# Collecting routed experts with sums taken in the last addition, squares on ScalarE and one Sqrt per step; the last W update left out

## The chip, the cores and the metric

The kernel runs on one core of a Trainium2 chip. All data are float32. The metric is the device time of that core in microseconds (us), and the time of a kernel is the median of its runs. For the kernel before it is 2762.55 us, the median of 3 runs between 2755.8 and 2763.34 us. One further execution was recorded by the hardware profiler: it took 2751.21 us, and its profile spans 2749.3 us of that.

## The reference

The input is 2 sequences of 4096 tokens of width 512. Two layers follow each other, each closed by a residual sum and a layer norm.

The first layer ("attention") is a recurrence per sequence. With k, v and q three projections of each token, it holds a matrix W (512x512) and a bias b, and per token computes

```
g = 2/512 * (W @ k + b - v)
W = W - 0.01 * outer(g, k);   b = b - 0.01 * g
out = W @ q + b
x = layernorm(x + out)
```

Only `out` leaves the recurrence. The W and b that stand after the last token are used by nothing.

The second layer is a mixture of 8 experts with hidden width 256. Every token goes through a shared expert, and through the 2 experts of 8 for which sqrt(softplus(logit)) is largest, weighted by that value:

```
y = shared(x) + sum over the 2 chosen e of  c_e * (silu(x @ W1_e + b1_e) @ W2_e + b2_e)
out = layernorm(x + y)
```

A layer norm here subtracts the mean of the 512 values of a token and divides by the root of their variance plus 1e-5.

## The kernel before, in words

**Steps.** The recurrence is done in 32 steps of 128 tokens of both sequences (`step(c)`, c = 0 to 31, lines 392 to 470). Within a step the 128 token updates are solved at once: `prep(c)` projects K and Q and forms small 128x128 matrices (L304, L317), `invert(c)` inverts their 32x32 diagonal blocks on VectorE (L347), `join(c)` joins the blocks to the full inverse in levels. A level is four matmuls into `pz` (L384) and one VectorE addition that gives the tile Z (L386); the next level multiplies Z again, so it can't start before that addition has ended. The last Z is called Y. Then come the right side R (L402 to L412), the output `po` (L422), transposes of K (`pk`, L437, copied to K by VectorE, L439), the solved update `pe` = Y times R (L446), F as its scaled copy by ScalarE (L448), the output's second part (L452), and the update of W (matmuls `pw` L457, additions L458) and of the bias (`pb` L463, L464).

**Shared expert and router.** `shared(c)` (lines 555 to 632) runs one step later: transposes, the shared expert, the router, whose activations are Exp, Ln, Silu and Sqrt on ScalarE, and a write of x plus the shared part to a DRAM table `gb`, which is the base that the routed experts are added to.

**Routed experts.** Steps 0 to 22 are group a and steps 23 to 30 group b. When a group's last step has been routed, `plan` sorts its tokens by expert into tiles of 128 rows. `routed(gr)` (lines 764 to 830) works the tiles off, 99 for a and 39 for b. Per tile k, GpSimd issues two gathers by DMA, the tokens `g` (L771) and the expert's weights `wb` (L777, 3 buffers, so those of tile k+3 wait until tile k has been read by the VectorE addition `o`, L809). TensorE transposes the tokens (`pg` L786; copied to gT by ScalarE, L788), multiplies (`phe` L795), ScalarE applies Silu (`he` L799), and TensorE multiplies again (`pye` L806). The result goes to the DRAM table `ge`.

**Collecting.** `collect(gr)` (lines 832 to 873) finishes the output of one step of the group at a time: `fetch` issues on GpSimd's queue the load of the base `acc` (L839, 3 buffers) and four gathers of routed rows, `z` (L845, 2 buffers each). VectorE adds the four weighted rows (L862, two per sequence); then `layernorm` (lines 273 to 291) does for each of the two sequences bn_stats (L276), bn_aggr (L278), an addition of eps (L280), Sqrt on ScalarE (L281), a reciprocal (L283), a product (L286) and the normalizing Identity on ScalarE (L287). ScalarE's queue then issues the write of `acc` to the output (L872). `fetch` for the next collected step is issued ahead of a collected step's additions.

**The last step's tokens** (c = 31) go through all 8 experts without sorting, in `dense` (lines 649 to 681), at the end.

**What sets the order.** The order of instructions on TensorE and VectorE is the order in which the program is written (L884 says so); the order on the other engines is chosen by the scheduler of the language. `interleave` (L63) mixes several generators: each yields an amount of work, and the one that is furthest behind its share goes on. In steps 28 to 31 group a's collecting is one of the parts, with an amount from `COLLECTED` (5, 5, 5 and 3 collected steps) and held back for the first part of the step (L900, L901). After step 31, tiles of b, the shared part of step 31 and the rest of a's collecting are mixed (L910); at the very end `dense` and the collecting of b (L913).

Of the kernel before, what the change touches and what calls it, by code (L numbers as in the profile page):

```python
# [40 lines left out]
F32 = mybir.dt.float32  # L41
# [60 lines left out]
def postln_block(ctx: ExitStack, tc: tile.TileContext, x, xT, thK, thV, thQ, w0, b0, masks, blk,  # L102
# [289 lines left out]
    def step(c):  # L392
# [25 lines left out]
        for s in range(B):  # L418
# [13 lines left out]
            if s == 0:  # L432

                for r in range(B):
                    ps = ps_s.tile([P, DC, P], F32, tag="ps", name=f"pk_{c}_{r}")
                    for ec in range(DC):
                        nc.tensor.transpose(ps[:, ec, :], KQ[:, ec, r, 0, :], ident)  # L437
                    k = stepp.tile([P, DC, P], F32, tag="K", name=f"K_{c}_{r}")
                    nc.vector.tensor_copy(k, ps)  # L439
                    K.append(k)  # L440
                    if r == 0:
                        Y = next(levels)
                    yield 1.5
        for s in range(B):
            ps = ps_s.tile([P, D], F32, tag="ps", name=f"pe_{c}_{s}")
            nc.tensor.matmul(ps, Y[:, s, :], R[s], start=True, stop=True)  # L446
            f = stepp.tile([P, D], F32, tag="F", name=f"F_{c}_{s}")
            nc.scalar.mul(f, ps, -BETA)  # L448
            F.append(f)
            yield 3.0  # L450
        for s in range(B):
# [3 lines left out]
            for ec in range(DC):  # L455
                ps = ps_s.tile([P, D], F32, tag="ps", name=f"pw_{c}_{s}_{ec}")
                nc.tensor.matmul(ps, K[s][:, ec, :], F[s], start=True, stop=True)  # L457
                nc.vector.tensor_tensor(W[s][:, ec, :], ps, W[s][:, ec, :], ALU.add)  # L458
                if s > 0 and ec == 1:
                    next(norm[0])  # L460
                yield 1.0
            ps = ps_s.tile([P, D], F32, tag="ps", name=f"pb_{c}_{s}")
            nc.tensor.matmul(ps, ones, F[s], start=True, stop=True)  # L463
            nc.vector.tensor_tensor(brep[s], ps, brep[s], ALU.add)  # L464
            yield 1.0
# [183 lines left out]
    def dense(c):  # L649
# [4 lines left out]
        for e in range(E + 1):  # L654
            if e < E:
                w = dense_w[e]
                h_e[e] = stepp.tile([P, HC, T], F32, tag="F", name=f"hd_{e}")
# [106 lines left out]
    def routed(gr):  # L764
# [17 lines left out]
        def turn(k):  # L782
# [4 lines left out]
            gT[k] = gp.tile([P, DC, P], F32, tag="gT", name=f"gT_{gr.g}_{k}", bufs=1)  # L787
# [43 lines left out]

    def collect(gr):
# [18 lines left out]

        fetch(0)
        yield 2.0
        for j in range(gr.n):
# [4 lines left out]
            norm = []  # L859
            for s in range(B):  # L860
                for k in range(K):
                    nc.vector.scalar_tensor_tensor(acc[:, s, :], z[s * K + k],  # L862
                                                   gr.cw[:, j, s, k:k + 1], acc[:, s, :],
                                                   ALU.mult, ALU.add)
                    yield 0.8
                norm.append(layernorm(acc, "f", c, s, scalar=True))
                next(norm[s])
                yield 0.4
                if s > 0:
                    next(norm[s - 1])  # L870
            next(norm[B - 1])
            nc.scalar.dma_start(out=out[:, c * P:(c + 1) * P, :].rearrange("s p d -> p s d"),  # L872
                                in_=acc)
# [7 lines left out]
    COLLECTED = {NCH - 4: 5, NCH - 3: 5, NCH - 2: 5, NCH - 1: 3}  # L881
# [5 lines left out]
    for c in range(NCH):  # L887
# [11 lines left out]
        if c > spread[-1]:  # L899
            amount = COLLECTED[c] * COLLECT  # L900
            parts.append((1.5 * amount, held(part_of(collects[0], amount), 0.25 * amount)))  # L901
# [4 lines left out]
        if c == NCH - 2:  # L906
            dense_weights(2)
    dense_weights(1 + B + 2)
    next(tiles[1])
    interleave([(b.tiles * TILE, tiles[1]), (60.0, shared(NCH - 1)),  # L910
                ((a.n - sum(COLLECTED.values())) * COLLECT, collects[0])])
    dense_weights(E - len(dense_w))
# [70 lines left out]
```

## Time and profile before

The profiled execution took 2751.21 us and its profile spans 2749.3 us. The stages around the change, by the times at which their first matmuls start:

| stage | us from the span's start | length |
|---|---|---|
| a step without routed work (step 16) | 1011.0 to 1072.6 | 61.6 |
| step 28 | 2164.5 to 2235.8 | 71.3 |
| step 29 | 2235.8 to 2306.2 | 70.4 |
| step 30 | 2306.2 to 2381.6 | 75.4 |
| step 31 | 2381.6 to 2459.4 | 77.8 |
| tiles of group b, with the rest of a's collecting | 2459.4 to 2670.1 | 210.7 |
| dense experts, with the collecting of b | 2670.1 to 2749.3 | 79.2 |

Durations of instructions that matter, as means of the profile: the weighted addition (L862) 757 ns, bn_stats 687, bn_aggr 182, the eps addition 153, the reciprocal 157, the product L286 214, a Sqrt 203, a normalizing Identity 805, a load of ScalarE's function table 1283, an indirect DMA on GpSimd about 1000 to 1075 with 300 between two, and the direct load of acc 767.

How to read it: PE is TensorE, PEld its weight loads, DVE VectorE, ACT ScalarE, POOL GpSimd. A table of stretches gives for each stretch its length, then busy time (and instructions) of PE, PEld, DVE, ACT and POOL, the granted share of TensorE's clock, the DMA engines' busy share and GB/s. In a timeline, each line is a start, a duration, engine, line and operation; a bracket at the end is the idle time before it and what ended it. In a list of waits, "A <- B: t, n, m" says that A waited for B for t us in total, n times, at most m.

### The profile page before, as it was taken

Reading aid. Unit: us, or ns where it says so; the run is one execution under the profiler, and the core shown is the slowest. Engines: PE = TensorE matmul, PEld = TensorE weight load, DVE = VectorE, ACT = ScalarE, POOL = GpSimd, SP = SyncE. Lnnn points to the kernel's source line nnn. Section 1 sums busy time; section 2 is a strip of 40 time slices with the busy share of each in tenths; the row PEclk is TensorE's granted clock in tenths of the full one; section 3 lists DMA queues with packets and bytes.
Section 4 is the critical chain, followed back from the end, with each engine's and each line's share of the span. In section 5 each row is a group of like instructions: output and inputs, shape, how many; then the busy total and the mean of one; then the engine's idle time right before and its main releaser. Section 6 shows DMA issues by size and latency. Waiting matters only on the chain.

```text
span 2749.3 us, 31544 instructions
## 1 busy us (share of the span) xinstructions
PE 2629.7 (96%) x10593; PEld 1683.8 (61%) x10593; DVE 1327.9 (48%) x4189; ACT 767.4 (28%) x1493; POOL 763.5 (28%) x767
## 2 busy tenths in 40 slices
PE   8999999999999999999999999999999989878886
PEld 6656666666656666666555766767676655445664
DVE  2455554455555555454556223232232588753228
ACT  1222222222222222232222322323133233414447
POOL 0111111111111111112113333342333354454445
PEclk9999999999999999999999999999999999889998
DMA  4112111111111111111113343452434365575566
GB/s 162 36 64 63 48 41 49 40 40 40 42 61 47 42 42 47 40 40 40 46 57 112 113 108 97 115 163 82 122 99 96 117 193 181 188 248 170 194 208 225
DMA packets 148785, 269.38 MB, mean 98 GB/s; under 512 B 61180, under 2 KB 62940, under 8 KB 145040
## 3 DMA queue, kind: packets, MB, share of 16 engines
q1 hardware_dynamic: 90608, 139.50, 15.5%
q0 software_dynamic: 49584, 111.61, 14.1%
q10 hardware_dynamic: 8432, 16.25, 1.6%
q8 instruction: 85, 1.39, 0.2%
q14 instruction: 76, 0.62, 0.1%
HBM read 333.37 MB, written 88.64 MB: 153 GB/s over the span
## 4 chain that ended last, share of the span: by engine, by line
PE 85%; DMA 4%; issue 4%; DVE 4%; ACT 2%; POOL 1%; SPq 0%; POOLq 0%; DVEq 0%; ACTq 0%
PE pkq L304 16%; PE pye L806 8%; PE pr L402 8%; PE pr L407 8%; PE po L422 8%; PE phe L795 7%; PE pw L457 7%; PE ph L582 4%; PE py L621 4%; PE pa L317 3%; PE pb L463 2%; PE pg L786 2%; PE po L452 2%; PE pe L446 2%; PE pz L384 1%
## 5 line engine op out<-in xcount | busy, mean ns | idle before, releaser
L347 DVE SCALAR_TENSOR_TENSOR X<-L,X 128x31 f32<-128x31 f32 (+22 forms) x1472 | 330.9, 270 | 26.2 <-DMA L<-dL 9.2
L795 PEld LDWEIGHTS phe<-gT,wb 128*128 128x128 f32 x2208 | 270.9, 194 | 66.0 <-issue 61.9
L809 DVE TENSOR_TENSOR o<-pye,wb 128x512 f32<-128x512 f32 x138 | 95.4, 691 | 424.3 <-PE pye L806 409.1
L806 PE MATMUL pye<-wb,he 128*128 128x512 f32 x552 | 269.8, 612 | 28.6 <-ACT he L799 20.5
L795 PE MATMUL phe<-gT,wb 128*128 128x128 f32 x2208 | 273.6, 278 | 11.9 <-DMA wb<-wcat_in,widx 10.4
L549 POOL DMA_INDIRECT gt<-code,ri x124 | 123.8, 998 | 548.9 <-DVE ri L546 518.5
L457 PE MATMUL pw<-F,K 128*128 128x512 f32 x512 | 246.8, 605 | 8.7 <-DVE x L453 6.8
L304 PE MATMUL pkq<-xT,thQ 128*128 128x256 f32 x1024 | 245.6, 384 | 9.8 <-DVE Z L386 9.8
L304 PE MATMUL pkq<-xT,thK 128*128 128x256 f32 x1024 | 243.6, 382 | 7.4 <-DMA thK<-thK_in 7.4
L422 PE MATMUL po<-W,kq 128*128 128x512 f32 x512 | 245.9, 604 | 0.0
L304 PEld LDWEIGHTS pkq<-xT,thK 128*128 128x128 f32 x1024 | 195.9, 192 | 71.6 <-issue 49.0
L402 PE MATMUL pr<-thV,xT 128*128 128x512 f32 x512 | 239.3, 599 | 0.0
L777 POOL DMA_INDIRECT wb<-wcat_in,widx x138 | 142.4, 1032 | 347.9 <-DVE o L809 191.7
L407 PE MATMUL pr<-W,kq 128*128 128x512 f32 x512 | 231.9, 592 | 0.0
L304 PEld LDWEIGHTS pkq<-xT,thQ 128*128 128x128 f32 x1024 | 187.2, 191 | 36.1 <-DVE Z L386 10.3
L799 ACT ACTIVATE he<-phe,wb 128x128 f32<-128x128 f32 x276 | 86.4, 363 | 417.0 <-PE phe L795 359.5
L458 DVE TENSOR_TENSOR W<-pw,W 128x512 f32<-128x512 f32 x256 | 173.5, 688 | 57.0 <-PE pw L457 52.9
L311 ACT COPY kq<-pkq 128x256 f32<-128x256 f32 x256 | 83.1, 375 | 390.3 <-PE pkq L304 383.9
L806 PEld LDWEIGHTS pye<-wb,he 128*128 128x128 f32 x552 | 99.2, 191 | 131.6 <-issue 90.2
L771 POOL DMA_INDIRECT g<-gy,gidx x138 | 138.5, 1004 | 146.2 <-PE pg L786 109.5
L457 PEld LDWEIGHTS pw<-F,K 128*128 128x128 f32 x512 | 94.0, 191 | 136.2 <-issue 96.7
L845 POOL DMA_INDIRECT z<-ge,sidx x124 | 133.3, 1075 | 117.7 <-DVE acc L862 40.4
(199 smaller groups left out, 3446.5 us busy)
## 6 DMA issues: line engine op xcount, KB each, us to landing
ge<-o SPq DMA_DIRECT2D x138, 256.0 KB
xT<-xT_in SPq DMA_DIRECT2D x32, 512.0 KB
x<-x_in SPq DMA_DIRECT2D x32, 512.0 KB
L<-dL SPq DMA_DIRECT2D x128, 128.0 KB
gy<-x SPq DMA_DIRECT2D x31, 512.0 KB
gb<-x SPq DMA_DIRECT2D x31, 512.0 KB
acc<-gb POOLq DMA_DIRECT2D x31, 512.0 KB
y_out<-acc ACTq DMA_DIRECT2D x31, 512.0 KB
```

Of the source, the lines that this page charges most:

```text
L304: nc.tensor.matmul(ps[:, i].rearrange("p s t -> p (s t)"), th[:, dc, (ec + i) * P:(ec + i + 1) * P], xt[:, dc].rearrange("p s t -> p (s t) ...
L347: nc.vector.scalar_tensor_tensor(X[:, h, j + 1:], L[:, j + 1:, j], X[:, h, j:j + 1], X[:, h, j + 1:], ALU.mult, ALU.add)
L402: nc.tensor.matmul(ps, xt[:, dc, s, :], nthV_sb[:, dc, :], start=(dc == 0), stop=False)
L407: nc.tensor.matmul(ps, KQ[:, ec, s, 0, :], W[s][:, ec, :], start=False, stop=(ec == DC - 1))
L422: nc.tensor.matmul(ps, KQ[:, ec, s, 1, :], W[s][:, ec, :], start=(ec == 0), stop=False)
L457: nc.tensor.matmul(ps, K[s][:, ec, :], F[s], start=True, stop=True)
L458: nc.vector.tensor_tensor(W[s][:, ec, :], ps, W[s][:, ec, :], ALU.add)
L771: nc.gpsimd.indirect_dma_start(out=g_t[k], out_offset=None, in_=gr.y, in_offset=bass.IndirectOffsetOnAxis(ap=gr.gidx[:, k:k + 1], axis=0), ...
L777: nc.gpsimd.indirect_dma_start(out=wbuf[k % NW], out_offset=None, in_=wcat, in_offset=bass.IndirectOffsetOnAxis(ap=gr.widx[:, k:k + 1], ax ...
L795: nc.tensor.matmul(ps[:, hc, :], w[:, dc * HF + hc * P:dc * HF + (hc + 1) * P], t[:, dc, :], start=(dc == 0), stop=(dc == DC - 1))
L806: nc.tensor.matmul(ps, h[:, hc, :], w[:, O2 + hc * D:O2 + (hc + 1) * D], start=(hc == 0), stop=(hc == HC - 1))
L845: nc.gpsimd.indirect_dma_start(out=t, out_offset=None, in_=gr.ex, in_offset=bass.IndirectOffsetOnAxis(ap=gr.sidx[:, j, s, k:k + 1], axis=0 ...
```

## The change

In `collect`, sums come out of the second weighted addition of a sequence itself (`accum_out`), the squares and their sums from two ScalarE activations, and eps, Sqrt, reciprocal and product are done for both sequences at once. The part from eps on is a generator, `finish`, that runs among the additions of the collected step after it. A flag, `squares`, turns this off for the stage of group b's tiles: there bn_stats and bn_aggr stay, still with one Sqrt, and VectorE does the normalizing.

In `step`, the last step has no transposes of K and no update of W and bias; the last level of `join` is issued ahead of the first transposes of K in every step; F takes the place of R. In `dense` a tile takes R's buffers in place of F's; gT has 2 buffers in place of 1. `COLLECTED` falls from 5, 5, 5, 3 to 3, 3, 3, 1 collected steps, and the collecting's amount and hold in a step change.

```diff
                 for r in range(B):
+                    if r == 0:
+                        Y = next(levels)
+                    if c == NCH - 1:
+                        continue
                     ps = ps_s.tile([P, DC, P], F32, tag="ps", name=f"pk_{c}_{r}")
                     for ec in range(DC):
                         nc.tensor.transpose(ps[:, ec, :], KQ[:, ec, r, 0, :], ident)
                     k = stepp.tile([P, DC, P], F32, tag="K", name=f"K_{c}_{r}")
                     nc.vector.tensor_copy(k, ps)
                     K.append(k)
-                    if r == 0:
-                        Y = next(levels)
                     yield 1.5
...
-            f = stepp.tile([P, D], F32, tag="F", name=f"F_{c}_{s}")
-            nc.scalar.mul(f, ps, -BETA)
-            F.append(f)
+            nc.scalar.mul(R[s], ps, -BETA)
+            F.append(R[s])
...
-            for ec in range(DC):
-                ps = ps_s.tile([P, D], F32, tag="ps", name=f"pw_{c}_{s}_{ec}")
...
+            if c < NCH - 1:
+                for ec in range(DC):
+                    ps = ps_s.tile([P, D], F32, tag="ps", name=f"pw_{c}_{s}_{ec}")
...
+            elif s > 0:
+                next(norm[0])
...
-            gT[k] = gp.tile([P, DC, P], F32, tag="gT", name=f"gT_{gr.g}_{k}", bufs=1)
+            gT[k] = gp.tile([P, DC, P], F32, tag="gT", name=f"gT_{gr.g}_{k}")
...
+        def finish(c, acc, mean, var, on_scalar):
+            if on_scalar:
+                nc.vector.tensor_scalar(var, var, 1.0 / D, EPS, ALU.mult, ALU.add)
+            else:
+                nc.vector.tensor_scalar(var, var, EPS, None, ALU.add)
+            nc.scalar.activation(var, var, AF.Sqrt)
+            yield
+            nc.vector.reciprocal(var, var)
+            if on_scalar:
+                nc.vector.tensor_tensor(mean, mean, var, ALU.mult)
+            for s in range(B):
+                if on_scalar:
+                    nc.scalar.activation(acc[:, s, :], acc[:, s, :], AF.Identity,
+                                         bias=mean[:, s:s + 1], scale=var[:, s:s + 1])
+                else:
+                    nc.vector.tensor_scalar(acc[:, s, :], acc[:, s, :], mean[:, s:s + 1],
+                                            var[:, s:s + 1], ALU.subtract, ALU.mult)
+            nc.scalar.dma_start(out=out[:, c * P:(c + 1) * P, :].rearrange("s p d -> p s d"),
+                                in_=acc)
+            yield
...
+            on_scalar = squares[0]
+            mv = sm.tile([P, 2, B], F32, tag="fmv", name=f"fmv_{c}")
+            mean, var = mv[:, 0], mv[:, 1]
+            for i in range(B * K):
+                s, k = i // K, i % K
+                nc.vector.scalar_tensor_tensor(
+                    acc[:, s, :], z[i], gr.cw[:, j, s, k:k + 1], acc[:, s, :], ALU.mult, ALU.add,
+                    accum_out=mean[:, s:s + 1] if on_scalar and k == K - 1 else None)
+                if i % 2 == 1:
+                    next(done, None)
+                yield 0.9
+            if on_scalar:
+                nc.vector.tensor_scalar(mean, mean, -1.0 / D, None, ALU.mult)
+                for s in range(B):
+                    nc.scalar.activation(z[s * K], acc[:, s, :], AF.Square,
+                                         bias=mean[:, s:s + 1], accum_out=var[:, s:s + 1])
+            else:
+                for s in range(B):
+                    st = sm.tile([P, 6], F32, tag="fst", name=f"fst_{c}_{s}")
+                    nc.vector.bn_stats(st, acc[:, s, :])
+                    nc.vector.bn_aggr(mv[:, :, s], st)
+            done = finish(c, acc, mean, var, on_scalar)
+            yield 0.4
+        for _ in done:
+            pass
...
-    COLLECTED = {NCH - 4: 5, NCH - 3: 5, NCH - 2: 5, NCH - 1: 3}
+    COLLECTED = {NCH - 4: 3, NCH - 3: 3, NCH - 2: 3, NCH - 1: 1}
...
-            parts.append((1.5 * amount, held(part_of(collects[0], amount), 0.25 * amount)))
+            parts.append((2.5 * amount, held(part_of(collects[0], amount), 0.6 * amount)))
...
+    squares[0] = False
     interleave([(b.tiles * TILE, tiles[1]), (60.0, shared(NCH - 1)),
                 ((a.n - sum(COLLECTED.values())) * COLLECT, collects[0])])
+    squares[0] = True
```

More of the change, by code (lines that the diff above doesn't have):

```diff
@@ L454, in step @@
             yield 2.0
-            for ec in range(DC):
-                ps = ps_s.tile([P, D], F32, tag="ps", name=f"pw_{c}_{s}_{ec}")
[L457 to L460, printed above, removed]
+            if c < NCH - 1:
+                for ec in range(DC):
+                    ps = ps_s.tile([P, D], F32, tag="ps", name=f"pw_{c}_{s}_{ec}")
+                    nc.tensor.matmul(ps, K[s][:, ec, :], F[s], start=True, stop=True)
+                    nc.vector.tensor_tensor(W[s][:, ec, :], ps, W[s][:, ec, :], ALU.add)
+                    if s > 0 and ec == 1:
+                        next(norm[0])
+                    yield 1.0
+                ps = ps_s.tile([P, D], F32, tag="ps", name=f"pb_{c}_{s}")
+                nc.tensor.matmul(ps, ones, F[s], start=True, stop=True)
+                nc.vector.tensor_tensor(brep[s], ps, brep[s], ALU.add)
                 yield 1.0
[L462 to L465, printed above, removed]
+            elif s > 0:
+                next(norm[0])
             norm.append(layernorm(y, "a", c, s))
@@ L656, in dense @@
                 w = dense_w[e]
-                h_e[e] = stepp.tile([P, HC, T], F32, tag="F", name=f"hd_{e}")
+                h_e[e] = stepp.tile([P, HC, T], F32, tag="R", name=f"hd_{e}")
                 for hc in range(HC):
@@ L830, in routed @@
             yield 2.0
+    squares = [True]
     def collect(gr):
@@ L850, in fetch @@
             got[j] = acc, z
+        def finish(c, acc, mean, var, on_scalar):
[18 more added lines that the diff above has]
+            yield
         fetch(0)
         yield 2.0
+        done = iter(())
         for j in range(gr.n):
@@ L858, in collect @@
             acc, z = got.pop(j)
[L859 to L873, printed above, removed]
+            on_scalar = squares[0]
[23 more added lines that the diff above has]
+            pass
     TILE, COLLECT, SHARED, PLAN, DENSE = 4.5, 4.0, 13.5, 10.0, 64.0
```

## The prediction

> **What bounds the kernel now.** I read the page's busy shares and slices first, then a table of stretches cut at the steps, the waits in each stretch, and timelines at the places where the diff reorders something.
>
> ```profile
> PE 2629.7 (96%) x10593; PEld 1683.8 (61%) x10593; DVE 1327.9 (48%) x4189; ACT 767.4 (28%) x1493; POOL 763.5 (28%) x767
> PE   8999999999999999999999999999999989878886
> PEclk9999999999999999999999999999999999889998
> ```
>
> TensorE is full up to slice 32 (some 2200 us) and has holes after it. So a VectorE instruction saved earlier is worth nothing, and a TensorE stall earlier costs its full length. The stretches (the rows are step 16; steps 28, 29, 30; step 31; tiles of b; dense):
>
> ```profile
> 1011.00:1072.64 61.64, 61.64 (x223) 37.95 (x222) 32.52 (x111) 14.29 (x27) 9.98 (x10) 1.00 0.14 45
> 2164.50:2235.80 71.30, 63.96 (x222) 38.62 (x222) 56.57 (x172) 23.44 (x45) 37.72 (x37) 0.98 0.57 156
> 2235.80:2306.20 70.40, 63.85 (x223) 38.59 (x222) 59.64 (x181) 24.77 (x48) 36.08 (x36) 0.98 0.61 191
> 2306.20:2381.60 75.40, 66.71 (x223) 40.34 (x222) 59.48 (x181) 24.86 (x48) 36.10 (x37) 0.93 0.68 219
> 2381.60:2459.40 77.80, 56.40 (x151) 28.18 (x151) 51.92 (x178) 17.36 (x31) 30.87 (x31) 0.85 0.55 175
> 2459.40:2670.10 210.70, 181.56 (x979) 127.13 (x978) 61.04 (x137) 89.93 (x174) 98.96 (x97) 0.97 0.60 204
> 2670.10:2749.30 79.20, 58.10 (x193) 36.46 (x191) 60.66 (x148) 57.69 (x80) 40.47 (x38) 0.90 0.65 216
> ```
>
> Steps 28 to 30 have step 16's matmuls (222 or 223) but last 71.3 + 70.4 + 75.4 - 3 x 61.64 = 32.2 us longer: VectorE is busy 57 to 60 us in each. In the tiles stretch VectorE is busy only 61 of 211 us; the waits there are others:
>
> ```profile
> PE pye L806 <- ACT he L799: 14.4, 8, 6.1
> PE phe L795 <- DMA wb<-wcat_in,widx: 6.3, 4, 3.2
> POOL acc L839 <- DMA y_out<-acc: 4.7, 1, 4.7
> ```
>
> In the dense stretch ScalarE repeats every 8.0 us (writes of y_out are issued at 2711.59 and 2719.59), without pause:
>
> ```profile
> 2712.88 0.47 ACT L664 ACTIVATE hd<-pd,b1e 128x256 f32<-128x256 f32 x1
> 2713.37 1.28 ACT L281 ACT_TABLE_LOAD   x1
> 2714.66 0.20 ACT L281 ACTIVATE frs<-frs 128x1 f32<-128x1 f32 x1
> 2714.88 1.28 ACT L664 ACT_TABLE_LOAD   x1
> ```
>
> **What the Trainium skill says.** "ScalarE: Activation LUTs", What ACT_TABLE_LOAD costs: 1283 ns per switch of set plus a drain; the trace has 1283 ns. The same page, Table sets, puts cheap functions such as copy and identity in every set; Square isn't named there, and no run shows it. "TensorE: Matmul & The Clock Gate", What's actually happening: about 3.4 us of idleness halve TensorE's clock; the trace agrees (after a gap of 3.28 us at 2344.4 eight pkq matmuls took 3.39 us, elsewhere 1.89). "VectorE: DVE Perf Modes", Two Vector instructions with no wait between them: an accumulator output is a second instruction; the trace has none.
>
> **The change part by part.** A minus is a gain.
>
> *Last join level ahead of the transposes (steps 0 to 27): +9 us.* This is the order in step 16:
>
> ```profile
> 1043.93 0.61 PE L384 MATMUL pz<-Z,N 128*128 128x128 f32 x4
> 1044.37 0.60 PE L596 MATMUL pht<-ident,pre 128*128 128x128 f32 x4
> 1044.58 0.42 DVE L386 TENSOR_TENSOR Z<-pz,DT 128x256 f32<-128x256 f32 x1 [3.38 <-PE pz L384]
> 1044.81 0.60 PE L437 MATMUL pk<-ident,kq 128*128 128x128 f32 x4
> 1045.25 0.61 PE L384 MATMUL pz<-Z,N 128*128 128x128 f32 x4
> ```
>
> The last pz now starts at 1045.25, behind pk, and Z is ready at 1045.00. Moved ahead of pk it would start at 1044.81, and so waits for Z: 0.24 us with the signal, up to 0.45 with a weight load that can't be drawn ahead; I take 0.35. TensorE is in order and full, so nothing hides it. Steps 1 to 23 have this order: 23 x 0.35 = 8; step 0 has no pht and loses 0.7; steps 24 to 27 have phe and pg (2.2 us) as cover and lose nothing. Ends +5 and +11.
>
> *Collecting in steps 28 to 30: -21 us.* Per collected step VectorE now does 4 x 0.757 + 2 x (0.687 + 0.182 + 0.153 + 0.157 + 0.214) = 5.8 us; after, 4 x 0.757 + four small ones of 0.16 + two accumulator reads (0 to 0.2 each; I take 0.15, like the smallest row) = 4.0. Per step: 29 us become 12, beside the 32.5 of step 16. Five collected steps sat in two thirds of a step (41 us, own work 0.53 x 41 = 22): 51 us of VectorE in 41, too much by 10, about what each step lost. Three sit in 0.4 of it (24.6 us): 12 + 13 = 25, no excess, and the additions to W behind it are free. What is late next is `acc`: it has 3 buffers, and its write now leaves one collected step later, during the additions of the next. The third load in a step then waits for a write only just issued, and VectorE behind it; with what Z loses I leave 3.5 us per step: 32.2 - 10.5 = 21.7. Ends -28 and -12.
>
> *Last W update dropped, one collected step in step 31: -12 us.* From the first pw at 2447.39 to the first pg at 2459.38 only one po of 0.86 remains: 11.1 us. Two pk save about 1, the collected steps that leave some 2 of the 3.7 us that pz waits for Z. Against that, the tiles start sooner and may wait for their first gathers, whose indices are ready at 2437.5: 2 us. Ends -16 and -6. In the trace their cover is the W update itself.
>
> *Tiles of b, with 13.5 collected steps in place of 5.5: +10 us.* Undisturbed a tile takes 4.22 us: 39 x 4.22 = 165, and the shared part of step 31 adds 11: 176; 35 are lost today. About 10 go to the router (pye waits 6.1 for ScalarE at 2485.8). A Sqrt puts two table loads, 2.8 us, between Silus and costs pye about 1.5; now two per collected step, then one: 13.5 x 1.5 = 20. On GpSimd a collected step is 0.77 + 4 x 1.0 plus gaps of 0.3: 6.3 us, ahead of `wb` of coming tiles; the 6.3 us of waits for wb per 5.5 collected steps become 15 per 13.5. Sum 176 + 10 + 20 + 15 = 221. VectorE has 6.3 us per collected step (it normalizes there), 85 + 27 for o, of 221: cover enough. Ends -10 and +45: GpSimd has 39 x 2.6 + 13.5 x 6.3 + 2.5 = 189 us of its own.
>
> *Dense stretch: 0.* ScalarE per collected step: now 4 loads 5.1 + 0.4 + Identities 1.5 + Silus 0.94 = 8.0, as seen. After: 2 loads 2.57 + Sqrt 0.2 + 1.5 + 0.94 + two Squares. He and hd (363 ns for 128, 472 for 256 columns, also with a bias) give 0.69 for 512; with 0 to 0.2 for the accumulator's read I take 0.8: together 6.8. But the buffers of acc close a loop over two periods: additions among pyd's 4.9, small ones 0.4, Identities 1.6, issue 0.4, write 3.7 (the last one) to 5.9 (2711.59 to the load at 2717.46), load and landing 6.5 (2696.27 to 2702.74): 17.5 to 19.7, so 8.7 to 9.8 us. The scheduler may hide some of it. Seven periods at 6.9 give -7, five at 9.8 give +9; I keep 8.0.
>
> *At nothing:* F in R's place (its readers come before R's next writer on TensorE; cover none needed), dense tiles in R's buffers (free since step 31), the second gT (pg follows phe on TensorE, so the copy never waited for it; at most 0.1 us a tile).
>
> Sum: 9 - 21 - 12 + 10 + 0 = -14 us on a span of 2749.3, which lies in an execution of 2751.2. The median shown, 2762.55, is 11 above that; I subtract from it: 2748. No change can't be told within 0.3%, 8.3 us.
>
> **Rivals.** (1) *The tiles stretch takes the collecting in its idle time*, since VectorE and GpSimd are idle more than half of it: no further waits for wb (206, so -5), and ScalarE's 6.9 us hold in the dense stretch (-7): 9 - 21 - 12 - 5 - 7 = -36, 2726. Against it stand 13.5 bursts of five DMAs. (2) *Slower: GpSimd's queue becomes the bound of the tiles stretch.* Each load of acc would wait on GpSimd for the write that frees its buffer, and gathers of wb and g stand behind it. In the whole run such waits are 7, 38.9 us; the one of this stretch took 4.7. 189 + 13.5 x 4.7 = 253, +42, in sum +19: 2781. It decides from 189 + 13.5w over 210.7 + 24 + 8 = 243, w = 4 us. For it: writes issued now just ahead of the loads. Against: a queue that is behind finds the writes landed. (3) *Square needs a table of its own:* two more loads per collected step, 2.57 us; in the dense stretch ScalarE then needs 9.4, +10: 2759, no change. That the sums aren't taken in the addition can't be: the code issues them.
>
> **How the numbers follow.** The likeliest case (2748, own range 2730 to 2758) has 0.52, rival 1 0.20, rival 2 0.18, rival 3 0.10. Faster by over 0.3%: 0.85 of the likeliest and rival 1, 0.64; the same: rival 3 and 0.13 of the likeliest, 0.17; slower: rival 2 and the rest, 0.19. The range 2710 to 2780 leaves out half of rival 2 and a few per cent below.
>
> **What would show it.** Step 16 some 0.3 us longer, pz waiting for Z; steps 28 to 30 at 64 to 66 us, VectorE under 48; the first pg 10 us nearer to the last pe; the tiles stretch at 215 to 228 with waits of wb and of acc for y_out; one Sqrt per collected step and no load ahead of a Square. Wrong if the tiles stretch passes 243 us, or stays under 205.

## The result, and the profile after

The changed kernel is slower: 2777.18 us median of 14 runs (2767.70 to 2785.89) against 2758.62 us for the kernel before (14 runs, 2750.33 to 2766.07). The ratio is 1.0070, with a 95% interval from 1.0055 to 1.0085. The profiled execution spans 2777.4 us, 28.1 more than the one of before. The forecast was 2748 us, faster.

The page of the changed kernel, first TensorE's busy share, then the slices and the granted clock:

```profile
PE 2633.1 (95%) x10565; PEld 1682.5 (61%) x10565; DVE 1287.2 (46%) x4079; ACT 754.6 (27%) x1498; POOL 758.8 (27%) x767
...
PE   8999999999999999999999999999999999787786
...
PEclk9999999999999999999999999999999999888998
```

VectorE has 41 us less to do than before, ScalarE 13 less, TensorE 28 matmuls less. None of that is the matter: the holes and the low clock at the end of the row PE have become deeper. The table of stretches of the changed kernel says where (step 16; steps 28, 29, 30; step 31; tiles of b; dense):

```profile
1016.99:1078.92 61.93, 61.76 (x222) 37.97 (x222) 32.68 (x111) 14.30 (x27) 9.93 (x10) 1.00 0.14 45
2177.52:2241.78 64.26, 62.27 (x222) 37.88 (x222) 43.10 (x133) 18.70 (x39) 26.75 (x28) 1.00 0.42 107
2241.78:2306.43 64.65, 62.14 (x222) 38.00 (x222) 41.83 (x141) 21.89 (x47) 25.90 (x26) 1.00 0.54 153
2306.43:2369.94 63.51, 62.07 (x223) 38.01 (x222) 41.98 (x141) 21.93 (x47) 24.97 (x25) 1.00 0.59 167
2369.94:2434.35 64.41, 47.61 (x123) 23.75 (x123) 30.21 (x131) 14.83 (x25) 22.06 (x21) 0.81 0.53 162
2434.35:2687.21 252.86, 195.09 (x980) 133.16 (x979) 103.92 (x221) 95.06 (x181) 135.55 (x135) 0.91 0.71 232
2687.21:2777.40 90.19, 62.35 (x193) 38.04 (x191) 45.38 (x119) 53.21 (x92) 40.61 (x39) 0.85 0.61 201
```

Against the table of before:

| term of the forecast's sum | before, us | after, us | forecast | traced |
|---|---|---|---|---|
| steps 0 to 27 | 2164.5 | 2177.5 | +9 | +13.0 |
| steps 28 to 30 | 217.1 | 192.4 | -21 | -24.7 |
| step 31 | 77.8 | 64.4 | -12 | -13.4 |
| tiles of b | 210.7 | 252.9 | +10 | +42.1 |
| dense | 79.2 | 90.2 | 0 | +11.0 |
| sum | 2749.3 | 2777.4 | -14 | +28.1 |

The tiles stretch grew by 13.5 us of TensorE's busy time (195.1 against 181.6, the same matmuls at a clock of 0.91 in place of 0.97) and by 28.6 us of TensorE's idle time (57.8 against 29.1). The waits in it:

```profile
POOL acc L846 <- DMA y_out<-acc: 27.9, 5, 9.9
PE pye L811 <- ACT he L804: 24.2, 14, 4.1
PE pg L791 <- DMA g<-gy,gidx: 11.7, 5, 6.4
PE phe L800 <- DMA wb<-wcat_in,widx: 9.2, 4, 3.2
```

Before, GpSimd waited here for `y_out` once, for 4.7 us, and TensorE never for `g`. The busy time that was added is what follows such a wait, as two lines of the timeline of the changed kernel show, one after a gap and one without:

```profile
2516.61 3.75 PE L800 MATMUL phe<-gT,wb 128*128 128x128 f32 x16 [3.25 <-DMA wb<-wcat_in,widx]
...
2525.72 2.07 PE L800 MATMUL phe<-gT,wb 128*128 128x128 f32 x16
```

The same 16 matmuls take 3.75 us in place of 2.07. "TensorE: Matmul & The Clock Gate" of the Trainium skill, What's actually happening, says that about 3.4 us of idleness halve TensorE's clock, and the trace agrees as far as it resolves this: the gap is 3.25 us and the factor 1.8. The forecast had named the page, but put no price on such gaps here.

In the dense stretch the period from one write of `y_out` to the next was 8.0 us. Now it is 9.3, 9.3 and 10.4 us (writes are issued at 2730.93, 2740.25, 2749.57 and 2759.97). Lines of one period, from the timeline of the changed kernel:

```profile
2736.60 1.34 POOL L852 DMA_INDIRECT z<-ge,sidx  x1 [3.25 <-DVE fmv L862]
...
2739.26 0.76 POOL L846 DMA_DIRECT2D acc<-gb  x1
...
2742.01 1.28 ACT L865 ACT_TABLE_LOAD   x1
...
2744.05 1.59 DVE L895 SCALAR_TENSOR_TENSOR acc<-z,cw,acc 128x512 f32<-128x512 f32 x2 [4.64 <-DMA acc<-gb]
...
2745.76 0.20 ACT L865 ACTIVATE fmv<-fmv 128x2 f32<-128x2 f32 x1 [2.47 <-DVE fmv L862]
2745.98 1.28 ACT L669 ACT_TABLE_LOAD   x1
...
2747.28 0.47 ACT L669 ACTIVATE hd<-pd,b1e 128x256 f32<-128x256 f32 x1
```

ScalarE no longer runs without pause: with half the table loads it waits 2.47 us for VectorE's addition of eps (L862), which stands behind the next collected step's additions; those wait 4.64 us for `acc`; and the load of `acc` went out at 2739.26, behind gathers of `z` that had waited 3.25 us on GpSimd for a buffer. So a loop through buffers seems to set the period, no longer ScalarE's work; the experiments decide it.

### The profile page after: what moved, and what is told of

It reads as the page before. It is cut to its first block, busy times and chain, and to the rows that moved or that the text cites. A ratio compares the mean times of both kernels' runs of the same rounds, so it can differ in the third digit from the quotient of the medians.

```text
span 2777.4 us, 31332 instructions
## 1 busy us (share of the span) xinstructions
PE 2633.1 (95%) x10565; PEld 1682.5 (61%) x10565; DVE 1287.2 (46%) x4079; ACT 754.6 (27%) x1498; POOL 758.8 (27%) x767
## 5 line engine op out<-in xcount | busy, mean ns | idle before, releaser
L811 PE MATMUL pye<-wb,he 128*128 128x512 f32 x552 | 277.9, 627 | 42.6 <-ACT he L804 36.3
L800 PE MATMUL phe<-gT,wb 128*128 128x128 f32 x2208 | 274.1, 278 | 14.4 <-DMA wb<-wcat_in,widx 12.7
L460 PE MATMUL pw<-R,K 128*128 128x512 f32 x496 | 236.1, 599 | 2.2 <-DVE x L455 1.1
L304 PEld LDWEIGHTS pkq<-xT,thQ 128*128 128x128 f32 x1024 | 186.0, 190 | 28.6 <-issue 5.3
L460 PEld LDWEIGHTS pw<-R,K 128*128 128x128 f32 x496 | 90.7, 190 | 123.5 <-issue 99.5
```

The costliest lines, as they stand in the source:

```text
L304: nc.tensor.matmul(ps[:, i].rearrange("p s t -> p (s t)"), th[:, dc, (ec + i) * P:(ec + i + 1) * P], xt[:, dc].rearrange("p s t -> p (s t) ...
L800: nc.tensor.matmul(ps[:, hc, :], w[:, dc * HF + hc * P:dc * HF + (hc + 1) * P], t[:, dc, :], start=(dc == 0), stop=(dc == DC - 1))
L811: nc.tensor.matmul(ps, h[:, hc, :], w[:, O2 + hc * D:O2 + (hc + 1) * D], start=(hc == 0), stop=(hc == HC - 1))
```

## The experiments

Theories for what the change costs after step 31. **Theory 1**: `finish` runs among the additions of the next collected step, so a buffer of `acc` comes free later and its next load blocks GpSimd's queue. **Theory 2**: the eight collected steps moved behind step 31 cost what GpSimd has to issue for them, whatever the buffers. **Theory 3**: ScalarE, its table loads and its queue. For the steps 0 to 27: the order of the last join level. All ratios are to the kernel before, run beside it on the same chip. Where two ratios are subtracted, the half widths of their intervals are added in squares. The length of a stretch comes from the one profiled execution of a kernel. For the tiles stretch this is coarse: in three pairs of the kernels below whose programs differ only ahead of it, it has 252.9 and 242.7 us, 235.5 and 243.2, 232.7 and 242.3. A difference of 10 us there shows nothing by itself.

**The old order at the last join level.**

```diff
-                    if r == 0:
-                        Y = next(levels)
                     if c == NCH - 1:
+                        if r == 0:
+                            Y = next(levels)
                         continue
...
                     K.append(k)
+                    if r == 0:
+                        Y = next(levels)
```

> The changed kernel, with the last join level behind the first transpose of K again. If the 13.0 us of steps 0 to 27 come from the last pz waiting for Z, step 16 goes from about 62.0 back to 61.64 us, steps 0 to 27 from 2177.5 to 2164.5 to 2167, and the whole is 10 to 13 us faster than the changed kernel, that is about level with the kernel before plus 15. If they come from F in R's buffers instead, the steps stay at 62.0 and the whole is unchanged.

Ratio 1.0026 (1.0016 to 1.0036): 0.44% less than the changed kernel, plus or minus 0.18%, that is 12 us, plus or minus 5. Steps 15 to 22 take 61.64 us again in place of 61.94, and steps 0 to 27 end at 2167.1. F in R's place is still there, so it is the order. The same place in step 16 of the changed kernel, answering to the five lines of before:

```profile
1049.92 0.61 PE L384 MATMUL pz<-Z,N 128*128 128x128 f32 x4
1050.37 0.60 PE L601 MATMUL pht<-ident,pre 128*128 128x128 f32 x4
1050.57 0.42 DVE L386 TENSOR_TENSOR Z<-pz,DT 128x256 f32<-128x256 f32 x1 [3.38 <-PE pz L384]
1051.14 0.68 PE L384 MATMUL pz<-Z,N 128*128 128x128 f32 x4 [0.17 <-DVE w L488]
1051.66 0.60 PE L441 MATMUL pk<-ident,kq 128*128 128x128 f32 x4
```

The last `pz` now starts at 1051.14, 0.77 us after `pht`, where it waits for Z. Before, `pk` started 0.44 us after `pht`, and `pz` 0.44 after that.

**A fourth buffer for acc** (gT goes back to one, which makes room).

```diff
-            acc = cp.tile([P, B, D], F32, tag="acc", name=f"acc_{c}", bufs=3)
+            acc = cp.tile([P, B, D], F32, tag="acc", name=f"acc_{c}", bufs=4)
...
-            gT[k] = gp.tile([P, DC, P], F32, tag="gT", name=f"gT_{gr.g}_{k}")
+            gT[k] = gp.tile([P, DC, P], F32, tag="gT", name=f"gT_{gr.g}_{k}", bufs=1)
```

> The changed kernel with a fourth buffer for acc (and one for gT, which makes room for it). Theory 1, the load of acc waits on GpSimd for the write that frees its buffer: the 34.1 us of waits for y_out in the tiles stretch fall under 10, that stretch goes from 252.9 to 215 to 230 us, the dense one from 90.2 to 80 to 85, the whole 25 to 45 us faster than the changed kernel. Theory 2, the number of DMAs that GpSimd issues (39 tiles and 13.5 collected steps, 189 us by the sum) sets the stretch whatever the buffers: it stays above 245 us, and waits for o or for z take the place of those for y_out. Theory 3, ScalarE's table loads and its queue: above 245 as well, with pye's waits for he at 24 us as they are.

Ratio 0.9948 (0.9930 to 0.9965), 1.2% below the changed kernel, some 34 us: theory 1's whole forecast. But the split was not as expected: the dense stretch fell from 90.2 to 74.4 us, the tiles stretch only to 235.5. Waits in the tiles stretch with four buffers:

```profile
PE pg L791 <- DMA g<-gy,gidx: 18.1, 8, 3.6
...
PE phe L800 <- DMA wb<-wcat_in,widx: 13.0, 5, 4.9
POOL acc L846 <- DMA y_out<-acc: 11.0, 2, 7.6
...
PE pye L811 <- ACT he L804: 7.4, 3, 4.1
```

The waits for `y_out` are down from 34.1 us (27.9, and 6.2 more that the profile books on `wb`) to 11.0; TensorE waits for gathers instead, 31.1 us in place of 20.9.

**Finishing at once**, three buffers as in the change.

```diff
-            done = finish(c, acc, mean, var, on_scalar)
+            for _ in finish(c, acc, mean, var, on_scalar):
+                pass
```

> The changed kernel with each collected step finished at once, not among the additions of the next: the write leaves some 8 us earlier. Theory 1: most of the waits for y_out go, the tiles stretch is 215 to 235 us; VectorE waits for ScalarE's Sqrt again, which costs 1 to 3 us in each of the steps 28 to 31; the whole 15 to 35 us faster than the changed kernel. Theories 2 and 3: the tiles stretch stays above 245 us and the whole is level or up to 8 us slower.

Ratio 1.0070 (1.0054 to 1.0087): the whole is level with the changed kernel, as theories 2 and 3 had it, but by two changes that cancel. After step 31 theory 1 holds: tiles 232.7 us, dense 79.9. But steps 28, 29 and 30 took 71.4, 71.3 and 71.5 us, 21.8 more than in the changed kernel, more than I had allowed.

**The late finish in the steps 28 to 31 only**, at once afterwards.

```diff
             done = finish(c, acc, mean, var, on_scalar)
+            if not late[0]:
+                for _ in done:
+                    pass
```

> The changed kernel, three buffers, with the finish among the next step's additions in the steps 28 to 31 only, and at once after them. If the late finish costs after step 31 and pays before it: steps 28 to 30 at 63 to 65 us as in the changed kernel, tiles and dense stretch together 310 to 322 us in place of 343, the whole 20 to 32 us faster than the changed kernel, ratio 0.995 to 0.9995. If the finish at once was only quicker because its tiles began later: the tiles stretch at 245 us or more and no gain.

Ratio 0.9986 (0.9977 to 0.9996): 0.84% (plus or minus 0.18) below the changed kernel, 23 us, by when the finish runs and nothing else. The steps keep 64.3, 64.9 and 63.5 us, tiles and dense come to 242.3 and 79.6. The late finish pays before step 31 and costs after it. What it costs there is more than the whole loss of 0.70%: without a fourth buffer, and with the new order still in, this kernel is no slower than the kernel before.

**No move**: five collected steps in each of the steps 28 to 30 and three in step 31, at the old pace, first with three buffers, then with four, then with three and Square writing into a tile of its own.

```diff
-    COLLECTED = {NCH - 4: 3, NCH - 3: 3, NCH - 2: 3, NCH - 1: 1}
+    COLLECTED = {NCH - 4: 5, NCH - 3: 5, NCH - 2: 5, NCH - 1: 3}
...
-            parts.append((2.5 * amount, held(part_of(collects[0], amount), 0.6 * amount)))
+            parts.append((1.5 * amount, held(part_of(collects[0], amount), 0.25 * amount)))
```

> The changed kernel with five collected steps in each of the steps 28 to 30 and three in step 31, at the pace of the kernel before: 8 collected steps leave the tiles stretch. Theories 1 and 2 both: the tiles stretch goes from 252.9 back to 200 to 215 us. Steps 28 to 31 take back a part of their gain: VectorE has 32.5 + 5 x 4.0 = 52.5 us per step in place of 57 to 60, so I expect 66 to 70 us per step, 12 to 25 us for the four. Together 15 to 30 us faster than the changed kernel, which is level with the kernel before or up to 10 us faster.

> The changed kernel with four buffers for acc (one for gT) and five collected steps in each of the steps 28 to 30, three in step 31, at the pace of before. With three buffers these steps took 79.7, 78.9 and 77.5 us, 8 more than with the old collecting. Theory 1, the late release of acc holds up GpSimd and then VectorE in these steps too: with four they take 65 to 71 us, the tiles stretch 200 to 210, the whole is 15 to 35 us faster than the kernel before. Rival, the Squares write into a z buffer and so hold up the next gathers of z, or VectorE simply has too much: the steps stay at 75 us or more, and the whole is level with the kernel before or slower.

> The changed kernel with five collected steps in each of the steps 28 to 30, as run before, but Square writes into a tile of its own and not into a z buffer. Theory, the Squares hold the z buffers, the gathers of z wait on GpSimd for ScalarE, and what stands behind them is late: the steps go from 79.7, 78.9 and 77.5 us to 68 to 73 us. Rival, the late release of acc or the work itself: they stay at 76 us or more.

Three buffers: 1.0104 (1.0086 to 1.0122); four: 0.9974 (0.9966 to 0.9982); own tile: 1.0102 (1.0073 to 1.0131). The tiles stretch went back to 210.2, 210.2 and 213.2 us, as both theories said. The steps were the surprise. Stretches of steps 28 and 29 with three buffers, and, from its timeline, the end of step 28 (a load of `acc`, the addition that needs the collected data, and the matmul that waits for the W update behind it):

```profile
2173.62:2253.30 79.68, 68.03 (x223) 39.95 (x222) 48.52 (x153) 26.03 (x54) 38.40 (x38) 0.91 0.56 157
2253.30:2332.20 78.90, 65.75 (x223) 38.89 (x222) 49.50 (x165) 30.93 (x64) 35.99 (x36) 0.91 0.60 175
```

```profile
2235.95 0.76 POOL L846 DMA_DIRECT2D acc<-gb  x1 [2.11 <-DMA y_out<-acc]
...
2243.22 0.75 DVE L895 SCALAR_TENSOR_TENSOR acc<-z,cw,acc 128x512 f32<-128x512 f32 x1 [6.59 <-DMA L<-dL]
...
2244.62 1.22 PE L466 MATMUL pb<-R,ones 128*128 128x512 f32 x1 [6.86 <-DVE W L461]
```

VectorE is busy 49 us per step, 8 to 10 less than before with as many collected steps, and yet the steps are 8, 8 and 2 us longer. VectorE stands 6.59 us in front of an addition (the profile books this on `L`), and TensorE stands 6.86 us behind that. With four buffers the steps take 75.0, 72.4 and 75.7 us; a tile of its own for Square takes 77.0, 75.6 and 77.1. So the late release seems to cost here too, some 4 us per step, and Square's hold on a z buffer some 2; the latter rests on one execution in the profile. Together that is about the 6 us per step by which these steps are longer than before, but no run has both repairs, so that they add up is not shown. With four buffers the steps are still 2 us longer than before each, and the whole lies between the two forecasts.

**The parts in the kernel before**: the move alone, the dropped W update alone, and both. The edits are those of the diff, with the collecting and the order left as they were.

> The kernel before with the move alone: three collected steps in each of the steps 28 to 30 and one in step 31, at the new pace; the collecting itself as it was. Theory 1 (the late finish is what costs): the tiles stretch takes the eight more collected steps at 210.7 + 8 x 1.5 to 2.5 = 222 to 232 us, without long waits of acc for y_out; the steps 28 to 30 take 63 to 66 us as in the changed kernel, so that their gain comes from the move and not from fewer VectorE operations; the dense stretch stays at 78 to 82; the whole is 5 to 20 us faster than before. Theory 2 (the count of DMAs on GpSimd): the tiles stretch takes 240 us or more, the whole is slower than before by 0 to 15 us.

> The kernel before without the last update of W and b and the two transposes of K in step 31, and nothing else. If the 11.1 us of these matmuls on TensorE are saved whole: 10 to 13 us faster than before (ratio 0.995 to 0.9965). If the tiles of b then wait for their first gathers, whose indices come no sooner: 6 to 9 us. If a later stretch takes it back: less than 5.

> The kernel before with the move and the dropped W update, the collecting itself and the order of the last join level as before. It differs from the changed kernel with the old order (ratio 1.0026) by the new collecting alone, with three buffers. If the new collecting with its late write is what costs: 0.996 to 1.000, the tiles stretch at 235 to 245 us and the dense one at 79 to 81 in place of 92. If the move with the drop is what costs: 1.001 to 1.004.

The move alone: 0.9991 (0.9980 to 1.0002), between both forecasts: steps 68.0, 65.0 and 65.0 us (19.2 less than before), tiles 237.7 us, 27 more. The drop alone: 0.9999 (0.9989 to 1.0009), nothing: step 31 is 15.5 us shorter, the tiles stretch 18.1 longer. Both: 0.9984 (0.9974 to 0.9993). In the kernel with the drop alone, two lines of GpSimd and one of TensorE at the start of the tiles (which begin at 2442.48) read:

```profile
2441.06 1.01 POOL L852 DMA_INDIRECT z<-ge,sidx  x1 [0.30 <-issue]
2453.45 0.77 POOL L846 DMA_DIRECT2D acc<-gb  x1 [11.38 <-ACT he L806]
```

```profile
2452.08 0.65 PE L575 MATMUL pt<-ident,x 128*128 128x128 f32 x2 [3.42 <-DVE x L289]
```

The gathers of the coming tiles stand behind a load of `acc` that waits 11.38 us, a wait that the profile books on ScalarE. In the kernel before this load had waited 9.19 us, for `y_out`, and went out at 2454.10, ahead of the tiles' start at 2459.4; now it goes out at the same time, but 11 us after the tiles' start. That is a part of the 18 us only. TensorE waits 12.4 us for `wb` in this stretch, where it had waited 6.3; the transposes of x wait 3.42 us for the layer norm of step 31, which had run beside the W update and now has nothing to run beside; and the same matmuls take 4.7 us more, at a clock of 0.96 in place of 0.97.

The third of these differs from the changed kernel with the old order by the new collecting, and by F in R's place and the second gT, which no run sets apart. Their tiles and dense stretches, first with the old collecting, then with the new one:

```profile
2432.00:2672.87 240.87, 188.32 (x978) 128.27 (x979) 101.21 (x247) 150.69 (x242) 138.72 (x136) 0.95 0.72 244
2672.87:2752.70 79.83, 59.83 (x193) 36.89 (x191) 60.06 (x147) 57.71 (x80) 40.40 (x38) 0.88 0.66 218
```

```profile
2424.95:2667.61 242.66, 187.97 (x979) 130.61 (x978) 103.70 (x221) 95.11 (x181) 136.25 (x135) 0.94 0.73 243
2667.61:2759.70 92.09, 65.17 (x193) 38.80 (x191) 45.12 (x119) 53.21 (x92) 40.39 (x39) 0.84 0.59 197
```

The tiles stretch is as long in both, 240.9 and 242.7, although ScalarE is busy 150.7 us in one and 95.1 in the other. But it is not long for the same reason. What TensorE waits for in it, again with the old collecting first:

```profile
PE pye L813 <- ACT he L806: 32.5, 18, 4.5
...
PE pg L793 <- DMA g<-gy,gidx: 2.3, 1, 2.3
...
PE phe L802 <- DMA wb<-wcat_in,widx: 2.1, 2, 1.3
```

```profile
PE pye L813 <- ACT he L806: 22.2, 13, 4.1
PE pg L793 <- DMA g<-gy,gidx: 14.1, 8, 4.9
PE phe L802 <- DMA wb<-wcat_in,widx: 13.8, 5, 4.2
```

With the old collecting TensorE waits for ScalarE's Silu and hardly for gathers; with the new one it waits 10 us less for ScalarE and 23 more for gathers. So the growth of this stretch from 210.7 us comes already with the move and the drop, and what the new collecting saves there on ScalarE it loses on late data. Theory 3 alone, ScalarE as what sets the stretch of the changed kernel, doesn't hold: 56 us less of ScalarE's work don't shorten it, and four buffers take the waits for `he` from 24.2 to 7.4 us with ScalarE's work unchanged. The dense stretch is where the new collecting loses, 12.3 us. In all it costs 0.42% with three buffers (1.0026 less 0.9984, plus or minus 0.14%).

**Old collecting, move, drop, and four buffers** (F in R's place makes room); and **new collecting, four buffers, old order**.

> The same with four buffers for acc (F in R's place makes room): the old collecting, the move, the dropped update. It differs from the changed kernel with four buffers and the old order (ratio 0.9913) by the new collecting alone. If the new collecting is worth its VectorE time once buffers are enough: 0.994 to 0.998, with the steps 28 to 30 one or two us longer each and the dense stretch at 78 to 80 us in place of 74.7. If the fourth buffer is what helps, whatever the collecting: 0.990 to 0.993.

> The changed kernel with four buffers for acc (one for gT) and the last join level behind the first transpose of K again. If the two repairs add up: 6 to 13 us faster than with the four buffers alone, ratio to the kernel before 0.990 to 0.993, with steps of 61.6 us, the tiles stretch at 230 to 238 and the dense one at 74 to 80. If one hides the other: 0.9945 or above.

0.9969 (0.9956 to 0.9981) and 0.9913 (0.9888 to 0.9937). With four buffers the new collecting gains 0.56% (plus or minus 0.28%), 15 us, where with three it lost 11.6. Fewer operations were worth something only once less waited for a buffer. A fourth buffer is not the only way to that: the kernel with the late finish in the steps only, at 0.9986, has three buffers and the new order; less the order's 0.44% it would stand near 0.994, an estimate from these ratios that no run shows, against 0.9984 with the old collecting. The old collecting has little use for the fourth: 0.15% (plus or minus 0.16). The last kernel, 2728.47 us against 2752.15, is faster than both kernels of the case. Its dense stretch takes 74.7 us, in its middle at periods of 6.5 to 7 us; its tiles stretch still takes 243.2:

```profile
2410.81:2653.96 243.15, 198.40 (x979) 135.84 (x978) 104.29 (x221) 95.44 (x181) 135.36 (x135) 0.89 0.73 243
```

**What is left in the tiles stretch.** Four further edits to that kernel or the changed one: the load of `acc` on SP's queue in the tiles stretch, with three and with four buffers; only one gather of `z` per sequence there; and four fewer collected steps there.

```diff
-            nc.gpsimd.dma_start(out=acc,
+            (nc.gpsimd if squares[0] else nc.sync).dma_start(out=acc,
```

```diff
                 for k in range(K):
+                    if k > 0 and not squares[0]:
+                        z.append(z[-1])
+                        continue
```

```diff
-    COLLECTED = {NCH - 4: 3, NCH - 3: 3, NCH - 2: 3, NCH - 1: 1}
+    COLLECTED = {NCH - 4: 4, NCH - 3: 4, NCH - 2: 4, NCH - 1: 2}
...
-            parts.append((2.5 * amount, held(part_of(collects[0], amount), 0.6 * amount)))
+            parts.append((2.0 * amount, held(part_of(collects[0], amount), 0.45 * amount)))
```

> The changed kernel with the load of acc issued on SP's queue in the tiles stretch; three buffers as they are. Theory 1, what costs is that this load blocks the gathers behind it on GpSimd: the stretch goes from 252.9 to 225 to 238 us, g and wb are no longer late for y_out. Rival, the wait costs where it lies: it now holds up the writes of o on SP, o has two buffers, and VectorE and TensorE wait for it; the stretch stays at 245 us or more.

> The changed kernel with four buffers for acc, the old order at the last join level, and the load of acc on SP's queue in the tiles stretch. With four buffers a cycle of that stretch is three tiles and one collected step in 15.3 us, of which GpSimd issues for some 14. Theory 2, GpSimd's issuing sets what is left: 1.07 us less per collected step, 13 of them, bring the stretch from 243 down by 8 to 16 us and the whole to a ratio of 0.986 to 0.989. If the bytes on the DMA engines set it: no change, 0.991 to 0.992.

> Four buffers for acc, the old order, and in the tiles stretch only one of the two gathers of z per sequence (its rows are added twice, so half of the routed rows is left out there): two DMAs of 1.3 us less on GpSimd per collected step. Theory 2, GpSimd's issuing: the stretch goes from 243 us down by 20 to 35 us, to 208 to 223. If ScalarE or VectorE sets it, whose work is unchanged: 238 us or more.

> Four buffers, the old order, and 4, 4, 4 and 2 collected steps in the steps 28 to 31 in place of 3, 3, 3 and 1: four fewer in the tiles stretch. If GpSimd's issuing sets that stretch at 3 to 4 us per collected step beyond what fits: 243 becomes 226 to 232 us, the steps take 65 to 69 us in place of 64, the whole ends at 0.989 to 0.993. If the collected steps don't set it: 238 us or more, and the whole 0.993 to 0.997.

On SP with three buffers: 1.0063 (1.0042 to 1.0085), the stretch at 246.8 us: gathers of `g` are no longer late (0.7 us), but SP now waits 75.8 us for `y_out`, and VectorE 17.2 us for writes of `o`, which SP issues. With four: 0.9931 (0.9906 to 0.9956), the stretch at 248.6: 11 DMAs less on GpSimd bought nothing (the profiled execution lies 16 us above the median, so the ratio counts here and not the length). Half the gathers of `z`, in a kernel that leaves out half of the routed rows there: one run of 2721.4 us, the stretch at 223.2. Four fewer collected steps: 0.9940 (0.9921 to 0.9959), not faster as a whole, since the steps 28 to 30 rose from 64.3, 64.1 and 64.1 to 71.8, 70.6 and 71.5 us. Its tiles stretch is the second line, that with half the gathers the first:

```profile
2420.92:2644.16 223.24, 187.11 (x979) 128.84 (x978) 103.97 (x221) 94.82 (x181) 112.15 (x111) 0.95 0.71 236
```

```profile
2437.42:2659.75 222.33, 185.07 (x978) 127.60 (x979) 81.30 (x173) 88.41 (x173) 119.97 (x117) 0.96 0.68 233
```

So the collected steps themselves make this stretch long, as theory 2 had it, some 5 us each by the last run (243.2 less 222.3, over four). More than half of that is TensorE's busy time, 198.4 us against 185.1 for the same matmuls, at a clock of 0.89 against 0.96: what a collected step costs there is in good part the slower clock behind the gaps. Whether the gaps come by GpSimd's issuing or by the bytes is not settled. The last column times the length gives what was moved: 43 MB before, 59 MB in the kernels with the move, 53 and 52 MB in these two, which are both about 20 us shorter. The load on SP, with less to issue on GpSimd and the same bytes, points to the bytes. It agrees with "DMA: Bandwidth & Descriptors" of the Trainium skill, Issuing engines are not separate DMA queues, that such a move saves only the time to start a transfer: 0.9931 against 0.9913 is no gain. But SP waited 73.4 us for `y_out` in that run, and the writes of `o` stood behind it, so that it doesn't decide.

**Four buffers with the late finish in the steps only**, and **four buffers with the W update kept**.

> Four buffers for acc, the old order, and the late finish in the steps 28 to 31 only. If the late release is still a cost with four buffers (11 to 15 us of waits for y_out stand in the tiles stretch there): ratio 0.986 to 0.990. If four buffers have done away with it: 0.990 to 0.993; if ScalarE's Sqrt in VectorE's way costs more in the dense stretch, up to 0.995.

> Four buffers and the old order, with the last update of W and its transposes done as before. If the tiles stretch waits for GpSimd however early it begins: step 31 is 10 to 14 us longer, the tiles stretch 8 to 16 us shorter, the whole within 0.990 to 0.993. If the dropped update is worth its 11 us here: 0.994 to 0.997.

The first: 0.9940 (0.9917 to 0.9963), no better than late everywhere (0.9913): with four buffers an early release gains nothing more. The second: 0.9982 (0.9973 to 0.9991), outside both forecasts: here the dropped update is worth 0.69% (plus or minus 0.26), 19 us. Step 31 is 9.3 us longer with it, and the tiles stretch no shorter (245.7 against 243.2); the rest of the 19 us is spread over other stretches and may be scatter.

## Why the prediction was wrong, point by point

**The last join level ahead of the transposes: right.** The forecast was 0.35 us in each of 23 steps plus 0.7 in step 0, so about 9 us. The steps show 0.30 us, and step 24 starts 8.5 us later (1514.34 against 1505.83). The other 4.5 us of the 13.0 lie in steps 24 to 27, where I expected none; the kernel with four buffers has the same order and takes 654.8 us there, before took 658.7, so that part is scatter between executions.

**Collecting in steps 28 to 30: the size right, the reason wrong.** -24.7 against -21. The step spoke of an excess of VectorE work, 51 us in 41, that fewer operations and fewer collected steps would remove together. With the old operations, three collected steps of 5.8 us would still have been too much by the same reckoning (17 + 13 in 24.6 us); yet the move alone gives 19.2 of the 24.7. The new operations add some 5.5 (198.0 us with the old collecting, move and drop, 192.5 with the new one and four buffers). And with the new operations but five collected steps, VectorE is busy 49 us and the steps are longer than before. What counts is how many collected steps lie in a step: with four buffers and the new collecting the three steps take 192.5, 213.9 and 223.1 us with three, four and five in each. The buffer loop seems to be a part of that, some 4 us per step with five of them; what the rest is was not isolated.

**Step 31: right in the trace, -13.4 against -12, but not as a gain of the whole.** In the kernel before, the same saving is gone again by the end of the tiles: waits for `wb`, the wait for step 31's layer norm and the slower clock take it back. The forecast had left 2 us for late gathers and nothing for the other two. Why the saving stays with four buffers and the new collecting, and doesn't with the old one, was not isolated.

**Tiles of b: mis-sized, +42.1 against +10. This is the step that failed most**, and 252.9 us is past the 243 that the forecast itself had set as the sign of being wrong. Term by term: waits of `pye` for ScalarE were to be 30 us (10 of the router, 20 of Sqrts) and are 24.2, so this term was about right; waits for `wb` were to be 15, and waits for `wb` and `g` are 20.9, those for `g` (11.7 us, before 0) not foreseen; other idle time was to be nothing and is 12.7. The largest miss is the first term, 176 us of undisturbed matmuls: they took 195.1 (before 181.6), since TensorE's clock is lower behind the gaps, and this had no term at all. By parts: the eight moved steps alone give +27, with the drop +30; the rest is the late release and scatter, which one trace each doesn't separate. That VectorE has cover enough there was true, and beside the point.

**Dense: +11.0 against 0.** The bound of the buffer loop was worked out, 8.7 to 9.8 us a period, and the measured periods are 9.3 to 10.4. It stood beside ScalarE's 6.9, and keeping 8.0 because the scheduler might hide some of it was the step that failed: here the longer of the two bounds held. With the loop eased by a fourth buffer the period is ScalarE's, 6.5 to 7; with the finish at once it is eased too, and the stretch takes 79.6 to 79.9 us. Square's hold on `z` is not what closes the loop: without the move and with three buffers the stretch takes 93.7 us with a tile of its own for Square, and 86.8 with Square in `z`.

**The rivals.** The second, GpSimd's queue, gave 253 us for the stretch and 2781 for the whole, and came within 4 us of the median (its terms add to +18, not +19). That the whole fits is in part luck: waits for `y_out` are 34.1 us over 13.5 collected steps, 2.5 each and below its own threshold of 4, it had no term for the slower clock, and it had 0 for the dense stretch. The first is refuted by the late gathers. The third is refuted: in the whole trace none of the 36 Squares has a table load just ahead of it.

Summed by ratios: the order +0.44%, the new collecting with three buffers (with F in R's place and the second gT) +0.42%, move and drop -0.16%; together +0.70%. These are differences along one chain of kernels, so they have to add up. What the forecast counted as a gain of 33 us in the steps 28 to 31 came as 38 in the traces, and the tiles stretch took nearly all of what the move and the drop had brought.

## What to carry to other kernels

When an edit delays the release of a buffer, work out the loop that this buffer closes (write, load, use), and take the longer of the loop's period and the engines' work as the forecast, not something between. Here an engine's busy time saved was worth nothing while its data came through such a loop: with one more buffer the same collecting went from 0.42% slower to 0.56% faster. When work is moved into a stretch whose engines look idle, count the DMAs that it brings there, and the gaps in TensorE's work that follow, with the lower clock after them.

## What was not expected of the hardware

A sum taken in the addition is nearly free: the accumulator's read is a second instruction and takes 83 ns (median of 36), where I had taken 150; the addition itself takes 748 ns with the sum and 745 without (medians of 36 and 88 in the changed kernel). ScalarE's read takes 188 ns behind a Square of 708 ns for 128x512.
